# Vision tower on one core: the tokenizer's first two units reordered, its first weights in one transfer, and unread products in five waits of TensorE

## The chip, the cores and the metric

The program runs on one core of a Trainium2 chip. The metric is the device time of one execution in microseconds (us). The core's engines are named as the profile names them: PE is TensorE (PEld its weight loads), DVE is VectorE, ACT is ScalarE, POOL is GpSimd, SP is SyncE, which here only issues transfers. Each engine works through its own list of instructions in order, and waits on semaphores for the others.

## The reference

128 images of 128 x 128 pixels pass through a tokenizer and two transformer layers, all in float32:

```python
# tokenizer
x = _bn(_conv(X, w1, 8), g1, b1, m1, v1)      # 8x8, stride 8, 64 channels
x = _bn(_conv(x, w2, 2), g2, b2, m2, v2)      # 4x4, stride 2, 256 channels
# layer 0, attention
diff = Qg - Kg
attn = jnp.einsum('bqkgd,d->bqkg', jax.nn.relu(diff), w_mlp) + b_mlp[0]
attn = jax.nn.softmax(jax.nn.relu(attn), axis=2)
# layer 0, 4 experts of attention, weighted by a softmax gate
attn = jax.nn.softmax(jnp.einsum('bcehtd,bcehsd->bcehts', q, k) * scale, axis=-1)
# layer 1, linear attention
attn_weights = jnp.einsum('bhnd,bhmd->bhnm', jax.nn.softmax(q, axis=-1), jax.nn.softmax(k, axis=-2))
# layer 1, 8 experts, one per token, at most C = 1280 tokens each
idx = jnp.argmax(probs, axis=-1)
hmid = jax.nn.relu(jnp.einsum('ecd,edf->ecf', buf, w1) + b1[:, None, :])
ybuf = jnp.einsum('ecf,efd->ecd', hmid, w2) + b2[:, None, :]
```

The four parts of the layers read a layer norm of h, and each is added to h.

The output has 128 x 64 tokens of 256 features. The tokenizer's output is reordered into an image and cut into patches, which fixes where each of its results is stored.

## The kernel before

The kernel runs six stages one after the other: `tokenizer` (lines 62 to 257), `relu_attention` (260 to 727), `expert_attention` (730 to 1081), `linear_attention` (1084 to 1436), `route` (1495 to 1617), which sorts tokens by expert, and `experts` (1620 to 1797). The activations `h2` stay in SBUF through the first three stages and go to DRAM (`hd`) at the end of the third.

**Order of the work.** A part of the code that stands under `with tc.manual_schedule():` keeps the written order on each engine. What stands outside such a region, all of `route` for example, is put in order by a planner, which gives an engine the first instruction, in the written order, that its own reckoning holds ready. Two regions that follow one another, as those of the blocks in `experts` do, keep their own order inside, and the planner decides how they interleave. Semaphores are added by the framework from what each instruction reads and writes; a tile buffer taken again waits for the last reader of what was in it.

**The tokenizer.** An image row of 8 pixel lines is one tile `xt` (512 KB); there are 16, loaded three ahead. `conv1(r)` multiplies row r by `w1bd`, the 64 x 64 first weights twice on the diagonal, in two products of 512 columns (L130), each into one of two PSUM buffers `pa`. ACT takes the first to `ev` (two instructions, L135), DVE the second to `h` (L132). `differences(r)` makes two more tiles of `h` on DVE (L141, L142). `between(m, i, k)` makes a tile `v`: minus a row on ACT (L151) where there is no row above, else the difference of two rows (L154). A `Unit(m, ab)` is one of 16 groups of results (row group m, 64 channels ab). It has three `products(i)`: 24 matmul instructions each (L177), then ACT (L189) and DVE (L200 or L204); `results(k)` writes `h2` (L210). Products 0 need v(m,0,0) and v(m,0,1), products 1 need rows 4m+1 and 4m+2, products 2 need v(m,2,0) and v(m,2,1). The second weights `w` come in two transfers of 512 KB on ACT's queue; POOL and ACT make sums and negatives of them (L223, L226, L227). Scales and offsets of the batch norms come from `bnv1` and `bnv2` (L107 to L111). Before the change rows 0 to 4 pass first, then units 0 to 15, each behind one more row while there are rows:

```python
            for r in range(5):
                conv1(r)
                ...
                differences(r)
            ...
            for m in range(4):
                for ab in range(4):
                    ...
                    if r < 16:
                        conv1(r)
                    u.products(0)
```

**The places of the unread products.** In `relu_attention` the last step of the last block ends with scores (L297), then a maximum, exponents, sums and weights on DVE, ACT and POOL (L521 to L535), then transposes on PE (L544), a copy (L552), and products with v in two halves (L441) with copies (L452) and transposes back (L459). At the start of `linear_attention` a group `x` of tokens is loaded (L1131), its statistics are taken (L1139, L1140, then POOL), and ACT normalises it in place:

```python
                nc.scalar.activation(
                    self.x[:, j], self.x[:, j], AF.Identity, bias=self.nb[:, j : j + 1], scale=self.rs[:, j : j + 1]
                )
```

PE then transposes it (L1159), and the products for queries and keys follow (L1182). In `route` PE transposes the logits `lgs` (L1533), waits while DVE finds each token's expert and counts (up to L1553), makes two small products `pp` (L1555, L1556), waits again, and makes 64 products `pi` in eight groups (L1604), for which DVE makes `lh` and `hv` (L1594, L1597; two buffers each) and ACT scales `hv` (L1602). In `experts` the tokens of a block are gathered by POOL's indirect transfers (L1681), normalised (L1691 to L1699), transposed (L1712, copied to `xt` by L1715), and multiplied by `w1` (L1724) and `w2` (L1740), block after block.

Of the kernel before, what the change touches and what calls it, by code (L numbers as in the profile page):

```python
# [19 lines left out]
P = 128  # L20
# [11 lines left out]
class Ctx:  # L32
# [12 lines left out]

    def tables(self, const):


        self.rin = const.tile([P, NTILE], I32, name="rin")
        self.rout = const.tile([P, NTILE], I32, name="rout")  # L50
        self.bexp = const.tile([P, NBLK + 1], I32, name="bexp")
# [10 lines left out]
def tokenizer(c, x, w1, bn1, w2, bn2):  # L62
# [6 lines left out]
    with (  # L69
# [16 lines left out]
        nc.vector.memset(w1bd, 0.0)  # L86
        bnv1 = wp.tile([P, 4], F32, name="bnv1")
        bnv2 = wp.tile([P, 4, 4], F32, name="bnv2")
        for k in range(2):
            nc.sync.dma_start(w1bd[k * 64 : (k + 1) * 64, k * 64 : (k + 1) * 64], w1)  # L90
            nc.sync.dma_start(bnv1[k * 64 : (k + 1) * 64, :], bn1)
# [8 lines left out]
        for k in range(2):  # L100
            nc.scalar.dma_start(bnv2[k * 64 : (k + 1) * 64], bn2)
# [44 lines left out]
        def between(m, i, k):  # L146
# [5 lines left out]
            else:  # L152
                eng = nc.vector if (m, k) == (0, 1) else nc.gpsimd
# [65 lines left out]
        with tc.manual_schedule():  # L219
            for r in range(5):  # L220
                conv1(r)
                if r == 1:
                    nc.gpsimd.tensor_add(w[:, :, 1], w[:, :, 0], w[:, :, 2])  # L223
                differences(r)
                if r == 1:
                    nc.scalar.mul(w[:, :, 2], w[:, :, 2], -1.0)  # L226
                    nc.gpsimd.tensor_add(w02, w[:, 0:2], w[:, 2:4])  # L227
                    between(0, 0, 0)
                elif r == 2:
                    between(0, 0, 1)  # L230
            for k in range(2):
                between(0, 2, k)
            s2, o2 = scale_offset(lambda i: bnv2[:, i, :], [P, 4], "2")
            n2 = wp.tile([P, 4], F32, name="n2")
            nc.vector.tensor_scalar_mul(n2, s2, -1.0)
            for m in range(4):
                for ab in range(4):
# [22 lines left out]
def relu_attention(c, wqkv, wmlp, bmlp):  # L260
# [8 lines left out]
    with (  # L269
# [387 lines left out]
        with tc.manual_schedule():  # L657
# [63 lines left out]
            old.weights()  # L721
            old.transpose()
# [361 lines left out]
def linear_attention(c, hd, hx, out, lgs, sth, wqk, bqk, wv, bv, wgb):  # L1084
# [6 lines left out]
    with (  # L1091
# [313 lines left out]
        with tc.manual_schedule():  # L1405
            for g in range(4):
                groups[g].load()
            for g in range(3):
# [86 lines left out]
def route(c, k, gfd):  # L1495
# [5 lines left out]
    with (  # L1501
# [54 lines left out]
        nc.tensor.matmul(pp[:, 1], k.ones, cs[:, T - 1, :], start=True, stop=True)  # L1556
        nc.vector.tensor_reduce(gf, sq, AX.X, ALU.add)
# [62 lines left out]
def experts(c, hx, gfd, out, w1, w2, b2, routing):  # L1620
# [9 lines left out]
    with ExitStack() as nest:  # L1630
# [138 lines left out]
        with tc.manual_schedule():  # L1769
            for n in range(2):  # L1770
                blocks[n].load()
            for n in range(2):
                blocks[n].gather((False,))
            blocks[0].moments()
# [49 lines left out]
def layout(**i):  # L1824
# [9 lines left out]
    o["w1"] = i["L0_tok_w1"].reshape(64, 64)  # L1834
    o["bn1"] = np.stack([i[f"L0_tok_{k}1"] for k in "gbmv"], axis=1)
# [5 lines left out]
    o["bn2"] = bn2.reshape(4, 8, 2, 8, 2).transpose(1, 3, 0, 2, 4).reshape(64, 4, 4)  # L1841
# [48 lines left out]
```

## Time and profile before

| what | value |
|---|---|
| median of 3 runs | 2775.22 us (2774.36 to 2785.34) |
| the profiled execution's own time | 2783.14 us |
| span of its profile (first to last instruction) | 2781.3 us |
| mean granted clock of PE | 0.965 |
| PE busy | 2609.6 us (94%) |
| PEld busy | 1748.0 us (63%) |
| DVE busy | 2036.5 us (73%) |
| ACT busy | 1627.1 us (59%) |
| POOL busy | 1628.1 us (59%) |

By stretches of the span, PE is busy and its clock is granted as follows:

| stretch, us | stage | PE busy, us | granted clock |
|---|---|---|---|
| 0 to 180 | tokenizer | 164.51 | 0.97 |
| 180 to 1114 | relu_attention | 906.48 | 0.99 |
| 1114 to 1948 | expert_attention | 806.37 | 0.98 |
| 1948 to 2284 | linear_attention | 297.88 | 0.92 |
| 2284 to 2346 | route | 28.58 | 0.52 |
| 2346 to 2781 | experts | 405.79 | 0.96 |

All times inside the execution are counted from the start of the span. A row of the timeline gives the start, the duration, the engine, the line, the operation and its tiles, how many instructions were merged, and in brackets how long the engine had been idle and what ended that. The granted clock is the share of full speed at which the profile shows PE running. A float32 product appears as two matmul instructions.

### The profile page before, as it was taken

Reading aid. Unit: us, or ns where it says so; the run is one execution under the profiler, and the core shown is the slowest. Engines: PE = TensorE matmul, PEld = TensorE weight load, DVE = VectorE, ACT = ScalarE, POOL = GpSimd, SP = SyncE. Lnnn points to the kernel's source line nnn. Section 1 sums busy time; section 2 is a strip of 40 time slices with the busy share of each in tenths; the row PEclk is TensorE's granted clock in tenths of the full one; section 3 lists DMA queues with packets and bytes.
Section 4 is the critical chain, followed back from the end, with each engine's and each line's share of the span. In section 5 each row is a group of like instructions: output and inputs, shape, how many; then the busy total and the mean of one; then the engine's idle time right before and its main releaser. Section 6 shows DMA issues by size and latency. Waiting matters only on the chain. (4 is left out here: it accounts for less than half of the span.)

```text
span 2781.3 us, 76925 instructions
## 1 busy us (share of the span) xinstructions
PE 2609.6 (94%) x33260; PEld 1748.0 (63%) x33260; DVE 2036.5 (73%) x3017; ACT 1627.1 (59%) x3411; POOL 1628.1 (59%) x1389
## 2 busy tenths in 40 slices
PE   7989999999999998899999999998899965999997
PEld 3553444444444443688888888887466645888886
DVE  6759999999998997577777777776467755444443
ACT  3228889888888887466665666565354432233332
POOL 3329888888888887765566565643133211454444
PEclk9999999999999999899999999999899975999999
DMA  3000000000000000000000000000444433555554
GB/s 107 31 12 1 2 1 2 1 2 2 1 2 1 2 2 2 12 11 18 11 18 11 11 18 11 18 11 17 115 89 109 101 90 109 173 191 190 194 194 133
DMA packets 138063, 140.80 MB, mean 51 GB/s; under 512 B 107923, under 2 KB 121509, under 8 KB 130032
## 3 DMA queue, kind: packets, MB, share of 16 engines
q1 hardware_dynamic: 126816, 117.91, 14.2%
q0 software_dynamic: 7648, 14.77, 1.7%
q8 instruction: 263, 4.31, 0.6%
q10 hardware_dynamic: 3248, 3.09, 0.4%
q14 instruction: 88, 0.72, 0.1%
HBM read 103.93 MB, written 32.54 MB: 49 GB/s over the span
## 5 line engine op out<-in xcount | busy, mean ns | idle before, releaser
L495 POOL TENSOR_TENSOR m<-q,k 128x1024 f32<-128x1024 f32 x384 | 719.0, 1903 | 30.5 <-PE sc L297 16.1
L487 DVE TENSOR_TENSOR m<-pc,k 128x2048 f32<-128x2048 f32 (+1 forms) x320 | 646.7, 2058 | 0.5 <-ACT q L431 0.5
L297 PE MATMUL sc<-m,wide 128*32 128x512 f32 x4096 | 529.6, 598 | 12.0 <-DVE m L487 7.1
L496 ACT ACTIVATE m<-m 128x1024 f32<-128x1024 f32 x384 | 402.2, 1049 | 5.9 <-POOL m L495 5.2
L297 PEld LDWEIGHTS sc<-m,wide 128*32 128x32 f32 x4096 | 126.4, 109 | 259.7 <-issue 146.2
L505 ACT ACTIVATE m<-k,q 128x64 f32<-128x64 f32 x1024 | 270.9, 339 | 0.8 <-DVE k L378 0.8
L946 DVE TENSOR_REDUCE mx<-sc 128x16 f32<-128x1024 f32 x128 | 156.1, 1220 | 154.7 <-PE sc L934 131.9
L961 POOL TENSOR_TENSOR e<-e,mx 128x1024 f32<-128x1024 f32 x128 | 243.4, 1902 | 10.1 <-POOL mx L960 0.2
L906 ACT COPY qk<-pqk 128x512 f32<-128x512 f32 x256 | 139.0, 605 | 134.3 <-PE pqk L902 134.3
L960 POOL TENSOR_TENSOR mx<-mx,gate 128x16 f32<-128x16 f32 x128 | 27.6, 216 | 316.9 <-ACT z L991 153.2
L1724 PE MATMUL ph<-xt,w1s 128*128 128x256 f32 x896 | 203.3, 386 | 3.4 <-DVE xt L1715 3.0
L1740 PE MATMUL po<-w2s,hT 128*128 128x256 f32 x896 | 198.0, 379 | 0.0
L973 ACT COPY pT<-pt 128x512 f32<-128x512 f32 x256 | 138.8, 600 | 98.9 <-PE pt L970 98.1
L1724 PEld LDWEIGHTS ph<-xt,w1s 128*128 128x128 f32 x896 | 173.3, 194 | 29.2 <-DVE xt L1715 3.8
L1740 PEld LDWEIGHTS po<-w2s,hT 128*128 128x128 f32 x896 | 168.1, 190 | 21.7
L902 PE MATMUL pqk<-xT,w 64*128 64x128 f32 x2048 | 169.5, 289 | 2.7 <-issue 2.7
L947 DVE TENSOR_TENSOR e<-sc,mx 128x1024 f32<-128x1024 f32 x128 | 156.8, 1225 | 4.4
L1728 ACT ACTIVATE hT<-ph,w1s 128x256 f32<-128x256 f32 x224 | 93.3, 470 | 106.6 <-PE ph L1724 106.6
L1758 POOL DMA_INDIRECT out<-y,rout x56 | 56.7, 1013 | 168.6 <-ACT hT L1728 125.1
L953 DVE TENSOR_REDUCE mx<-e 128x16 f32<-128x1024 f32 x128 | 153.3, 1198 | 2.5 <-ACT e L950 2.4
L902 PEld LDWEIGHTS pqk<-xT,w 64*128 64x128 f32 x2048 | 142.3, 189 | 20.4 <-issue 11.1
L970 PE MATMUL pt<-ident,e 128*128 128x128 f32 x1024 | 142.9, 280 | 5.0 <-POOL e L961 1.5
(290 smaller groups left out, 4986.7 us busy)
## 6 DMA issues: line engine op xcount, KB each, us to landing
w1s<-in_we SPq DMA_DIRECT2D x30, 1028.0 KB, 5.3
w2s<-in_we SPq DMA_DIRECT2D x30, 1024.0 KB, 5.0
hd<-h SPq DMA_DIRECT2D x16, 512.0 KB, 3.2
x<-hd SPq DMA_DIRECT2D x16, 512.0 KB, 3.9
h<-hd SPq DMA_DIRECT2D x4, 2048.0 KB, 12.7
hx<-h SPq DMA_DIRECT2D x4, 2048.0 KB, 11.4
out<-h SPq DMA_DIRECT2D x4, 2048.0 KB, 20.6
xt<-in_x SPq DMA_DIRECT2D x15, 512.0 KB, 3.5
```

The source lines that it names most:

```text
L297: nc.tensor.matmul(dst[j : j + 32], wide[:, hf, s : s + 32], part, start=start, stop=stop)
L487: nc.vector.tensor_tensor(m, bcast(self.pq[:, hf, i : i + n], 3, T), k, ALU.max)
L495: nc.gpsimd.tensor_tensor(m, bcast(self.q[:, hf, s : s + 2], 3, T), k, ALU.subtract)
L496: nc.scalar.activation(m, m, AF.Relu)
L505: nc.scalar.activation(self.parts[i, hf][:, q], self.blk.k[:, hf, i], AF.Relu, bias=self.q[:, hf, i - NB // 2, q : q + 1], scale=-1.0,)
L902: nc.tensor.matmul(pq[par][:, k, eh, :], w[r, f : f + P], self.xT[r, fc], start=True, stop=True)
L946: nc.vector.tensor_reduce(mx, sc, AX.X, ALU.max)
L947: nc.vector.tensor_sub(e, sc, bcast(mx, 2, T))
L953: nc.vector.tensor_reduce(self.sm[x], self.e[x], AX.X, ALU.add)
L961: nc.gpsimd.tensor_mul(e, e, bcast(sm, 2, T))
L1724: nc.tensor.matmul(ph[:, j], self.w1[:, w0 : w0 + P], self.xt[:, fc], start=(fc == 0), stop=(fc == 1))
L1740: nc.tensor.matmul(po, self.hT[:, f, r * P : r * P + P], self.w2[:, f, :], start=(f == 0), stop=(f == 7))
```

## The change

A helper `busy(out, x, n)` multiplies the identity by x n times into a PSUM tile that nobody reads. It is called in five places: 4 products ahead of the tokenizer's first unit, 9 ahead of the last transposes of `relu_attention`, 6 at the start of `linear_attention`, 7 in `route` behind `pp`, and 12 at the start of `experts`. In the tokenizer the order is written out anew: units 0 and 1 begin after row 2, and rows 3 to 6 and the parts of the two units alternate. One of the differences of rows moves from DVE to POOL. The first weights arrive as a full 128 x 128 matrix laid out by the host, in one transfer and without a memset, `bn1` and `bn2` in one transfer each, and `bn2` on SP's queue.

```diff
@@ -42,6 +42,11 @@
         nc.vector.memset(self.nhalf, -0.5)
         self.zero = const.tile([P, 8], F32, name="zero")
         nc.vector.memset(self.zero, 0.0)
+
+    def busy(self, out, x, n):
+
+        for _ in range(n):
+            self.nc.tensor.matmul(out, self.ident, x, start=True, stop=True)
 
     def tables(self, const):
 
@@ -83,12 +88,10 @@
 
 
         w1bd = wp.tile([P, P], F32, name="w1bd")
-        nc.vector.memset(w1bd, 0.0)
         bnv1 = wp.tile([P, 4], F32, name="bnv1")
         bnv2 = wp.tile([P, 4, 4], F32, name="bnv2")
-        for k in range(2):
-            nc.sync.dma_start(w1bd[k * 64 : (k + 1) * 64, k * 64 : (k + 1) * 64], w1)
-            nc.sync.dma_start(bnv1[k * 64 : (k + 1) * 64, :], bn1)
+        nc.sync.dma_start(w1bd, w1)
+        nc.sync.dma_start(bnv1, bn1)
         load(0, nc.scalar)
         for r in range(1, 3):
             load(r)
@@ -97,8 +100,7 @@
         w02 = wp.tile([P, 2, 3, D], F32, name="w02")
         for k in range(2):
             nc.scalar.dma_start(w[:, :, 2 * k, :], w2[k].rearrange("k p c -> p k c"))
-        for k in range(2):
-            nc.scalar.dma_start(bnv2[k * 64 : (k + 1) * 64], bn2)
+        nc.sync.dma_start(bnv2, bn2)
 
         def scale_offset(bnv, shape, name):
 
@@ -150,7 +152,7 @@
             if r < 0:
                 nc.scalar.mul(v, parts[r + 2], -1.0)
             else:
-                eng = nc.vector if (m, k) == (0, 1) else nc.gpsimd
+                eng = nc.vector if (m, i, k) == (0, 0, 1) else nc.gpsimd
                 eng.tensor_sub(v, parts[r], parts[r + 2])
             taken[m, i, k] = v
 
@@ -217,24 +219,46 @@
                 )
 
         with tc.manual_schedule():
-            for r in range(5):
-                conv1(r)
-                if r == 1:
-                    nc.gpsimd.tensor_add(w[:, :, 1], w[:, :, 0], w[:, :, 2])
-                differences(r)
-                if r == 1:
-                    nc.scalar.mul(w[:, :, 2], w[:, :, 2], -1.0)
-                    nc.gpsimd.tensor_add(w02, w[:, 0:2], w[:, 2:4])
-                    between(0, 0, 0)
-                elif r == 2:
-                    between(0, 0, 1)
-            for k in range(2):
-                between(0, 2, k)
+            conv1(0)
+            conv1(1)
+            nc.gpsimd.tensor_add(w[:, :, 1], w[:, :, 0], w[:, :, 2])
+            differences(0)
+            nc.scalar.mul(w[:, :, 2], w[:, :, 2], -1.0)
+            differences(1)
+            nc.gpsimd.tensor_add(w02, w[:, 0:2], w[:, 2:4])
+            between(0, 0, 0)
+            conv1(2)
+            differences(2)
+            between(0, 0, 1)
             s2, o2 = scale_offset(lambda i: bnv2[:, i, :], [P, 4], "2")
             n2 = wp.tile([P, 4], F32, name="n2")
             nc.vector.tensor_scalar_mul(n2, s2, -1.0)
+
+            c.busy(ps1.tile([P, 4, B], F32, tag="pa", name="idle"), w[:, 0, 0:2], 4)
+            units = [Unit(0, ab) for ab in range(2)]
+            units[0].products(0)
+            conv1(3)
+            units[0].products(1)
+            differences(3)
+            units[0].results(0)
+            between(0, 2, 0)
+            conv1(4)
+            units[1].products(0)
+            differences(4)
+            between(0, 2, 1)
+            units[1].products(1)
+            units[1].results(0)
+            conv1(5)
+            units[0].products(2)
+            units[0].results(1)
+            differences(5)
+            between(1, 0, 0)
+            conv1(6)
+            units[1].products(2)
+            units[1].results(1)
+            differences(6)
             for m in range(4):
-                for ab in range(4):
+                for ab in range(0 if m else 2, 4):
                     u = Unit(m, ab)
                     r = 4 * m + 5 + ab
                     if r < 16:
@@ -719,6 +743,7 @@
             old.exponents()
             old.sums()
             old.weights()
+            c.busy(psq.tile([P, 8, T], F32, tag="pq", name="idle"), blocks[-1].k[:, 0, 0:8], 9)
             old.transpose()
             old.transposed()
             for n in range(len(seq), len(seq) + 12):
@@ -1405,6 +1430,7 @@
         with tc.manual_schedule():
             for g in range(4):
                 groups[g].load()
+            c.busy(psp.tile([P, 2, D], F32, tag="pp", name="idle"), groups[0].x[:, 0:2], 6)
             for g in range(3):
                 for i in range(NG):
                     groups[g].statistics(i)
@@ -1554,6 +1580,8 @@
         pp = gpp.tile([P, 2, E], F32, name="pp")
         nc.tensor.matmul(pp[:, 0], k.before, cs[:, T - 1, :], start=True, stop=True)
         nc.tensor.matmul(pp[:, 1], k.ones, cs[:, T - 1, :], start=True, stop=True)
+        idle = gpp.tile([P, 4, B], F32, name="idle")
+        c.busy(idle, k.lgs[:, 0], 7)
         nc.vector.tensor_reduce(gf, sq, AX.X, ALU.add)
         nc.vector.reciprocal(gf, gf)
         nc.scalar.dma_start(gfd.rearrange("(p t) o -> p (t o)", p=P), gf)
@@ -1771,6 +1799,7 @@
                 blocks[n].load()
             for n in range(2):
                 blocks[n].gather((False,))
+            c.busy(psh.tile([P, 2, BLK], F32, tag="ph", name="idle"), blocks[0].w1[:, 0:512], 12)
             blocks[0].moments()
             blocks[0].normal()
             blocks[0].transpose()
@@ -1831,14 +1860,17 @@
     ev, od = x[:, :, :, 0::2], x[:, :, :, 1::2]
     x = [np.concatenate(y, axis=2) for y in ((ev[:, 0], od[:, 0]), (od[:, 1], ev[:, 1]))]
     o["x"] = np.concatenate(x, axis=1)
-    o["w1"] = i["L0_tok_w1"].reshape(64, 64)
-    o["bn1"] = np.stack([i[f"L0_tok_{k}1"] for k in "gbmv"], axis=1)
+
+    o["w1"] = np.zeros((P, P), np.float32)
+    for k in range(2):
+        o["w1"][k * 64 : k * 64 + 64, k * 64 : k * 64 + 64] = i["L0_tok_w1"].reshape(64, 64)
+    o["bn1"] = np.tile(np.stack([i[f"L0_tok_{k}1"] for k in "gbmv"], axis=1), (2, 1))
 
     w2 = i["L0_tok_w2"].reshape(4, 4, 64, 8, 2, 8, 2).transpose(0, 1, 2, 4, 6, 3, 5).reshape(4, 4, 64, D)
     o["w2"] = np.stack([w2[:, 1::-1], w2[:, 3:1:-1]]).reshape(2, 4, P, D)
     bn2 = np.stack([i[f"L0_tok_{k}2"] for k in "gbmv"], axis=0)
 
-    o["bn2"] = bn2.reshape(4, 8, 2, 8, 2).transpose(1, 3, 0, 2, 4).reshape(64, 4, 4)
+    o["bn2"] = np.tile(bn2.reshape(4, 8, 2, 8, 2).transpose(1, 3, 0, 2, 4).reshape(64, 4, 4), (2, 1, 1))
     q, k, v = (i[f"L0_attn_W{n}"].T for n in "qkv")
 
     v = v.reshape(D, 32, 8).transpose(0, 2, 1).reshape(D, D)
```

## Prediction

> **What bounds the kernel now.** I read the stretches first (start and end, length, busy time and instructions of PE, PEld, DVE, ACT and POOL, granted PE clock, DMA share, GB/s), because products that nobody reads can act on the clock alone:
>
> ```profile
> 0.00:34.00 34.00, 18.59 (x23) 6.35 (x24) 15.75 (x23) 11.55 (x13) 12.04 (x16) 0.85 0.43 144
> ...
> 1098.00:1116.00 18.00, 8.55 (x308) 7.04 (x304) 7.49 (x21) 3.36 (x6) 2.89 (x9) 0.81 0.05 11
> 1948.00:1966.00 18.00, 6.63 (x16) 3.82 (x17) 6.70 (x27) 5.21 (x10) 6.75 (x24) 0.53 0.61 203
> 2283.00:2310.00 27.00, 1.38 (x8) 1.17 (x8) 19.49 (x81) 0.63 (x1) 0.00 (x0) 0.57 0.31 77
> 2318.00:2346.00 28.00, 27.59 (x128) 27.38 (x128) 13.44 (x15) 16.62 (x64) 0.00 (x0) 0.50 0.59 226
> 2346.00:2362.00 16.00, 7.46 (x20) 5.83 (x21) 5.31 (x18) 0.84 (x2) 12.16 (x14) 0.51 0.15 41
> 2362.00:2764.00 402.00, 398.33 (x1890) 349.30 (x1888) 177.20 (x414) 120.14 (x278) 196.53 (x225) 1.00 0.55 185
> ```
>
> In the last row, which is nearly all of `experts`, PE is busy 99% at full clock: there it is the bound, and a later start is a later end. The other rows are the surroundings of the five places. The largest piece of work at half clock is `pi` in `route`, 27.59 us of PE in 2318 to 2346. The waits of PE (total, times, longest) name what ends each place's wait:
>
> ```profile
> PE pp L1555 <- DVE cs L1553: 25.6, 1, 25.6
> PE pt L1159 <- ACT x L1150: 14.6, 4, 6.0
> ...
> PE pi L1604 <- ACT hv L1602: 8.1, 1, 8.1
> PE pt L1712 <- DVE xn L1699: 7.9, 1, 7.9
> ...
> PE pt L544 <- POOL e L535: 4.6, 1, 4.6
> ```
>
> Then the timeline of the tokenizer's start:
>
> ```profile
> 16.07 0.81 DVE L132 TENSOR_SCALAR h<-pa,s,o 128x512 f32<-128x512 f32 x1 [2.45 <-PE pa L130]
> 17.08 3.90 POOL L227 TENSOR_TENSOR w<-w 128x1536 f32<-128x1536 f32 x1 [4.87 <-ACT w L226]
> 17.63 3.91 DVE L142 TENSOR_TENSOR h<-h,ev 128x512 f32<-128x512 f32 x1
> 21.57 1.48 ACT L151 ACTIVATE v<-h 128x1536 f32<-128x1536 f32 x1 [4.56 <-DVE h L142]
> 34.73 2.81 PE L177 MATMUL pc<-v,w 128*64 128x256 f32 x24
> ```
>
> A 0.69 us difference on DVE takes 3.91 because POOL's L227 runs beside it. From 34.73 to 179.92 PE never stops, so that an earlier start of the units is worth only what it leaves less to do.
>
> **Prices.** A product of `busy` is two instructions 0.43 us apart at full clock, 0.86 a product (row 1.98 for 4, L130 at 42.65), and 1.71 at half (3.75 for 4 at 7.60; where one was cut by the clock, 0.85 an instruction). Full clock came back 3.3 us after PE began anew at 187.46 (granted from 190.8) and 6.1 us after 2355.63 (from 2361.7): I carry both ends. n products that begin at half clock take 0.86 n plus half the time to full clock, 1.7 to 3.1 us. All 38 run in front of real products on the same engine, so what outlasts a wait is delay.
>
> [...]
>
> **Tokenizer.** (a) `w1bd` goes first on SP, and `bnv1` second, at 1.41 after an issue of 0.61. Issue to landing was 2.9 to 5.6 for `bnv`, 4.5 to 5.4 for `w1bd`: I take bnv1 at 5.9 (5.2 to 6.3). Scales took 1.39 (7.74 to 9.13), the table load 1.28, `ev` 1.57: row 0 is on ACT until 10.3, before 12.08. (b) Row 1 at half clock: 1.71 to 12.05, ev until 13.65, L226 (1.06) until 14.75, L227 3.90 until 18.65: 2.3 earlier than the 20.98 of before. (c) Both rows' differences now stand behind row 1's L132 at 13.8, so that L227 catches the second of four; three end behind it, one every 0.6: 20.45. L151 until 22.0, row 2's ev until 23.6 (24.65 before). (d) The 4 unread products need the PSUM buffer that this ev frees, and PE has been idle since 17.2: they run 23.6 to 28.7 or 30.1. I take 29.5. The last `v` (h2, d2, 1.76) is ready at 26.7, so they outlast their wait by 2.8; without them the first unit would start at half clock and lose 1.7 to 3.1 itself. (e) Before, six rows were through at 34.73; now three, and a row between units costs 9.83 - 7.77 = 2.06 (unit with a row, 42.65 to 52.48, and without, 138.31 to 146.08). Break-even is 34.73 - 6.2 = 28.55: **+0.95**. (f) v(0,2,1) moves from DVE (1.76) to POOL (3.44) and stands behind v(0,2,0) there. From 29.5: unit 0's second product ends at 36.7, z 38.3, row 3's differences 39.5, POOL until 43.4 (with 0.4 lost to L210), row 4's differences, blocked until then, 44.6, POOL until 48.1. PE wants it at 46.0 (29.5 + 4 x 2.59 + 3 x 2.06): **+2.1**, with all later units queued behind it on PE. Sum **+3.1**; bounds +0.6 (clock still full at 23.6, start 27.1, same wait) and +4.0 (bnv1 at 6.3, slow return of the clock). At nothing: the memset (DVE idle until 7.74), two issues less on ACT (idle until 9.21), `bnv2` on SP behind rows 1 and 2 (first read at 26.8; the next issue there is row 3's, at 11.38 before). Without that cover each would cost its issue, 0.6.
>
> **relu_attention, 9 products.** They start at 1098.1 at full clock: 7.7 us, until 1105.8. The transposes were released at 1102.89. At full clock L552 follows them after 1.19 (1095.24 to 1096.43): 1107.0 for 1104.91. The first half of L441 takes 1.48 (row at 332.80) for 2.12. **+1.5** (0.9 if the second half gains too, 2.1 if nothing does); the next stage's memsets wait for the last L459.
>
> **linear_attention, 6 products.** They read the group that ACT normalises in place, so L1150 waits for the sixth: a wait added, with four normalisations, the transposes and L1160 behind it. Start 1955.3 (x landed), length 5.2 + 1.7 to 3.1: until 1962.2 to 1963.6 instead of L1150 at 1959.67. L1182 goes from 1962.94 to 1965.5 to 1966.9; at full clock, where before 2.86 us (until 1965.8) ran at half, worth 1.43. **+1.7** (2.5; 0 if the three later waits of L1159 for ACT, 8.6 us, swallow it).
>
> **route, 7 products.** `route` is ordered by the planner. It takes what is ready:
>
> ```profile
> 2293.68 0.82 DVE L1523 TENSOR_REDUCE var<-sth 128x64 f32<-128x512 f32 x1
> 2294.41 0.19 DVE L1519 TENSOR_SCALAR mean<-mean 128x64 f32<-128x64 f32 x1
> ...
> 2305.21 0.69 DVE L1557 TENSOR_REDUCE gf<-sq 128x64 f32<-128x512 f32 x1
> 2305.82 0.68 DVE L1548 TENSOR_REDUCE m<-oh 128x64 f32<-128x512 f32 x1
> ```
>
> L1557 is written behind `pp` (L1555) and runs 4 us ahead of it. The unread products need `lgs` alone, ready at 2278; I expect them right behind the transposes, 2283.6 to 2289.6, in the middle of a wait of 25.6 us: **0**, the clock is down again long before 2318. This is the point the time hangs on most.
>
> **experts, 12 products.** They begin at 2345.9, at half clock: 10.3 + 1.7 to 3.1, until 2357.9 to 2359.3; the transposes were released at 2353.76. Then 0.60 for 1.08 and 7.07 (row at 2391.37) for 10.16: the first hidden layer ends at 2366.2 to 2367.6 instead of 2365.79. Behind it PE waited 2.19 us at 2375.32 for `xt` (gathers that POOL issues one after the other), which covers that; and the wait cost the next L1724 8.86 for 7.07. With PE later this wait is too short to drop the clock: **-1.5** (-3.6 if the later load of w1 also lets the gather land sooner; +1.0 if the clock drops all the same).
>
> **The sum**: 3.1 + 1.5 + 1.7 + 0 - 1.5 = +4.8. The profiled execution's 2783.14 (span 2781.3 and 1.8 around it) would become 2787.9. It lies 7.9 above the median of 2775.22, one of whose runs was 2785.34; from the median the sum gives **2780**. Its bounds, -2.1 and +9.6, give 2773 to 2785. About 0.5%, 13.9 us, is what a measurement of this kernel can tell from no change: I forecast no change.
>
> **Rivals.**
> - *The products of route stay behind pp.* They would end at 2317.5 to 2318.9, with the clock full as `pi` begins. Its groups then go by DVE, ACT and two buffers (1.95 + 2.06 + 0.5 over 2, 2.28) instead of 3.42: eight end at 2336.2 for 2345.85, -9.6, and the 12 start at full clock, 10.3 for a wait of 8.0: -1.0. Sum -4.3: 2771 (bound -11.7, 2763.5). For it: the written place. Against: L1557.
> - *Both, and the tokenizer without its waits*: start at 27.1 and no wait in (f) is -1.4; with -9.6, -3.6 and places two and three at 0, 2760.6. Needs four ends at once.
> - *Slower.* The 12 products make the planner's PE late, and it puts the gather's statistics ahead of `xt` in more blocks. One such wait costs 2.19 and 1.8 at half clock, 4.0 together; with +4.8 it passes 13.9 from 3 of the 28 blocks left, and 8 give 2812. Against: L1715 delays L1724 in only two of 29 blocks.
> - *The unread products are dropped in compilation.* Then only the tokenizer counts, start 26.7 with 1.7 to 3.1 lost and the wait of (f): +2.7, 2778.
>
> **How the numbers follow.** Forecast 0.69; route in order 0.15; both 0.04; slower 0.06; dropped 0.06. 2766 to 2786 leaves out "both", "slower" and the tails of the first two, at most 0.2 together. Faster by over 0.5% takes the 0.04 and a tail, 0.06; slower the 0.06 and a tail, 0.07; the rest is within.
>
> **What would show it.** Right: the first L177 near 29.5, a PE wait for POOL's L154 of some 2 us near 46, L544 near 1105.8, L1150 near 1963, the products of route before 2290, a granted clock of 0.5 through `pi`, a full one from 2362 on. Wrong: `pi` at full clock, no wait near 46, or waits of L1724 for L1715 past 2400.

## The result and the profile after

The changed kernel has a median of 2790.5 us (16 runs, 2785.4 to 2796.0). The kernel before, with more runs than the three that were known when the prediction was made, has a median of 2782.7 us (16 runs, the three among them). The ratio is 1.0034, with a 95% interval from 1.0025 to 1.0043: slower, by less than the 0.5% that the prediction counted as a change. The forecast "no change" held by that bound; the predicted time of 2780.0 did not, and 2790.5 lies 4.5 us above the top of its range. The profiled execution of the changed kernel took 2789.33 us (span 2787.6), that of the kernel before 2783.14 (span 2781.3).

Line numbers have moved: by 2 in the first half of the tokenizer, by 24 to 28 from `relu_attention` on; `busy` is L49. The stretches of the kernel after, with the columns as before:

```profile
0.00:34.00 34.00, 22.54 (x78) 9.37 (x80) 15.68 (x26) 11.87 (x15) 9.62 (x16) 0.95 0.41 142
...
1948.00:1968.00 20.00, 11.59 (x26) 5.62 (x27) 6.81 (x28) 3.43 (x7) 7.04 (x25) 0.66 0.48 160
...
2324.00:2352.00 28.00, 27.48 (x129) 27.29 (x129) 13.41 (x17) 16.23 (x63) 0.00 (x0) 0.50 0.58 220
2352.00:2366.00 14.00, 13.64 (x28) 5.95 (x28) 2.83 (x10) 0.00 (x0) 9.12 (x10) 0.81 0.13 38
2366.00:2770.00 404.00, 400.41 (x1904) 351.00 (x1904) 178.85 (x421) 120.52 (x280) 199.86 (x228) 1.00 0.55 185
```

The first row shows a clock of 0.95 where it was 0.85. The third shows `pi` unchanged, 27.5 us at 0.50. The fourth is the wait ahead of `experts`, now full of unread products, and the last says that PE is the bound behind it, as before. The waits of PE:

```profile
PE pp L1581 <- DVE cs L1579: 20.5, 1, 20.5
PE pt L1184 <- ACT x L1175: 9.9, 7, 4.0
...
PE pi L1632 <- ACT hv L1630: 8.1, 1, 8.1
```

The wait ahead of `pp` is 5 us shorter, that ahead of `pi` is what it was: the products of `route` went to the front of the first one, between and behind the transposes of the logits. The timeline of the tokenizer's start (start, duration, engine, line, operation):

```profile
13.97 3.86 POOL L228 TENSOR_TENSOR w<-w 128x1536 f32<-128x1536 f32 x1 [1.17 <-ACT w L226]
14.48 3.90 DVE L144 TENSOR_TENSOR h<-h,ev 128x512 f32<-128x512 f32 x1
...
19.20 5.37 PE L49 MATMUL idle<-w,ident 128*128 128x512 f32 x8 [4.89 <-issue]
...
24.50 2.81 PE L179 MATMUL pc<-v,w 128*64 128x256 f32 x24
...
43.38 2.38 PE L179 MATMUL pc<-v,w 128*64 128x256 f32 x20 [1.67 <-POOL v L156]
```

The last of the four differences that stood in a row is caught by POOL's sum, as expected: it begins behind the sum and takes 3.90 us where one takes 0.68. The unread products start as soon as DVE has emptied a buffer (19.11), not when ACT has; the first unit starts at 24.50, and near 43 PE waits for POOL's second `v`. The two places that cost most of the rest:

```profile
1955.94 8.12 PE L49 MATMUL idle<-x,ident 128*128 128x512 f32 x12 [1.30 <-DMA x<-hd]
1964.80 0.33 PE L1184 MATMUL pt<-ident,x 128*128 128x128 f32 x1 [0.74 <-ACT x L1175]
...
1967.28 7.13 PE L1207 MATMUL pq<-w,xT 128*128 128x512 f32 x16 [0.24 <-ACT xT L1185]
...
2351.98 13.23 PE L49 MATMUL idle<-w1s,ident 128*128 128x512 f32 x24 [0.52 <-PE pi L1632]
```

Read as a ledger against the one trace of before, start against start: the tokenizer ends 2.1 us earlier; the stage behind `relu_attention` starts 0.6 later (+2.7); the first L1207 starts 4.3 later than the first L1182 did; `route` starts 5.6 later, `pi` 5.6 later, the end comes 6.3 later. The experiments showed that such a ledger of two single traces misleads by several us.

### The profile page after: what moved, and what is told of

Read it like the earlier page. It is cut to its first block, busy times and chain, and to the rows that moved or that the text cites. A ratio compares the mean times of both kernels' runs of the same rounds, so it can differ in the third digit from the quotient of the medians.

```text
span 2787.6 us, 77062 instructions
## 1 busy us (share of the span) xinstructions
PE 2634.8 (95%) x33336; PEld 1756.3 (63%) x33336; DVE 2035.3 (73%) x3015; ACT 1627.6 (58%) x3411; POOL 1634.0 (59%) x1390
## 5 line engine op out<-in xcount | busy, mean ns | idle before, releaser
L1752 PE MATMUL ph<-xt,w1s 128*128 128x256 f32 x896 | 199.0, 380 | 3.2 <-ACT hT L1756 1.6
L1752 PEld LDWEIGHTS ph<-xt,w1s 128*128 128x128 f32 x896 | 169.8, 190 | 28.0 <-ACT hT L1756 2.9
```

The source lines that it names most:

```text
L1752: nc.tensor.matmul(ph[:, j], self.w1[:, w0 : w0 + P], self.xt[:, fc], start=(fc == 0), stop=(fc == 1))
```

## The experiments

The expectations name theories by a letter: P is a term of the prediction, T the reading of that ledger, H two thresholds of the clock, W the offset of its windows (both the author's assumptions then; what the traces show of them stands in the last section), Q a meeting of POOL and DVE; the others are described where they stand. The median and the range are those of the kernel's runs; the ratio is to the kernel before, run beside them. Its median was 2781.9 us beside `tok_alone`, `places_alone`, `route_late` and `no_linear`, 2779.5 beside `no_experts` and the three `doses`, 2778.2 beside `no_relu` and `transfers_only`, 2782.2 beside the four `warm` kernels and 2779.3 beside the last two. The changed kernel's 2790.5 stood beside 2782.7, so that differences to it are good to some 3 us; where they matter, each median is also taken against that of the kernel before beside it.

**1. The tokenizer alone, and the four later places alone.** `tok_alone` drops the four later calls:

```diff
-            c.busy(psq.tile([P, 8, T], F32, tag="pq", name="idle"), blocks[-1].k[:, 0, 0:8], 9)
-            c.busy(psp.tile([P, 2, D], F32, tag="pp", name="idle"), groups[0].x[:, 0:2], 6)
-        c.busy(idle, k.lgs[:, 0], 7)
-            c.busy(psh.tile([P, 2, BLK], F32, tag="ph", name="idle"), blocks[0].w1[:, 0:512], 12)
```

> The changed kernel without the four later sets of unread products (9, 6, 7 and 12), so the tokenizer's part of the change alone. Theory T (the trace of after is the measure): PE leaves the tokenizer near 177.8 instead of 179.9, about 2 us are won and kept, so 1.7 to 2.1 us less than the kernel before, ratio 0.9993; relu_attention's last transposes begin near 1101.2 and pi runs at half clock as before. Theory P (my prediction's term): 3.1 us more than before, ratio 1.0011. Theory C (chance): places at the end of linear_attention where the clock drops or not differ from run to run by up to 3 us either way, so the time may lie 3 us to either side of T while the tokenizer's own end still shows 177.8.

Measured: 2783.0 (2775.4 to 2786.2), ratio 1.0007, interval 0.9996 to 1.0018, which is +1.9 us, from -1.1 to +5.0. P's +3.1 lies inside, T's -2 outside, although the trace of this kernel again ends the tokenizer 2.3 us ahead of before's. `places_alone` has the tokenizer of before and the four later calls:

> The kernel before with the four later sets of unread products, the tokenizer as before. T: relu_attention +2.0, start of linear_attention +2.7, route 0, experts +0.7, so 5.4 us more than before, ratio 1.0019; up to 3 us more or less by the clock at the end of linear_attention. P: +1.5, +1.7, 0, -1.5, so 1.7 us more, ratio 1.0006. The unread products of route run before 2290 and pi at a granted clock of 0.50 by both.

Measured: 2784.1 (2780.5 to 2792.7), ratio 1.0019, interval 1.0005 to 1.0032: +5.3 us, from +1.4 to +8.9 (+2.2 by the medians). That is near T's 5.4, but P's 1.7 lies inside too.

**2. One place left out.** `no_linear`, `no_experts` and `no_relu` are the changed kernel without one of the lines above.

> The changed kernel without the six unread products of linear_attention. T: the first L1207 begins at the time of before plus what stands ahead of it (near 1963.2) instead of 1967.3, its first 16 take 8.5 instead of 7.1, so 2.7 us less than the changed kernel (up to 3 us more or less by the clock at the end of linear_attention). P: 1.7 less. A third theory, that the later start only shifts later waits for ACT: within 1 us of the changed kernel.

Measured: 2787.2 (2783.3 to 2790.4), 3.3 less than the changed kernel; ratio 1.0027, interval 1.0013 to 1.0041.

> The changed kernel without the 12 unread products of experts. T (trace of after): the first L1752 begins at pi's end plus 9.8 as before, at half clock, the first hidden layer takes 10.2 and the second waits for xt as before: 0.7 us less than the changed kernel. P: 1.5 us more. Rival: the later load of PE changes the order of DVE's work in the blocks behind, and the time moves by more than 3 us either way.

Measured: 2787.7 (2784.8 to 2792.2), 2.8 less; ratio 1.0030, interval 1.0016 to 1.0044. P's 1.5 more is not seen.

> The changed kernel without the nine unread products of relu_attention. T: the last transposes start 3 us earlier but at half clock, the stage ends 2.0 us earlier relative to its start: 2 us less than the changed kernel's 2790.4. P: 1.5 less. Rival: the stage behind starts with waits for its weights and for POOL, which take it back: within 0.7 us of the changed kernel.

Measured: 2786.7 (2784.4 to 2790.7), 3.8 less; ratio 1.0029, interval 1.0017 to 1.0040. But with each median taken against the kernel before beside it, the three are 2.5 less, 0.5 more and 0.7 more than the changed kernel, and the intervals of the ratios overlap its own, 1.0025 to 1.0043. By the times, none of the three places is shown to cost anything; for two of them the stages below show it.

**3. The products of route behind pp.** In `route_late` they are written into the buffer of `pp`, so that they must wait for its readers:

```diff
-        pp = gpp.tile([P, 2, E], F32, name="pp")
+        big = gpp.tile([P, 4, B], F32, name="pp")
+        pp = big[:, 0, 0 : 2 * E].rearrange("p (a e) -> p a e", a=2)
...
-        c.busy(idle, k.lgs[:, 0], 7)
...
         nc.vector.tensor_add(cs, cs, bcast(pp[:, 0], 1, T))
+        c.busy(big, k.lgs[:, 0], 5)
```

> The changed kernel with five unread products of route in place of seven, written into the PSUM buffer of pp, so that they cannot run before DVE has read pp. They start near 2316.6, last 4.3 to 8.5 us, and pi begins near 2324. Theory H (the clock has two thresholds: kept at full while PE does some 0.4 of its possible column work in a window of 3.4 us, regained only above about 0.8): pi, which does 0.61 of it at half clock and would do about 0.46 when DVE sets its pace, stays at full clock: 27.6 becomes 18 to 20 us, and the 12 products behind it take 10.3 instead of 13.2, so 10 to 13 us less than the changed kernel, near 2779, ratio to before 0.9985. Rival: one threshold between 0.61 and 0.8 for both ways: the clock falls within pi after one window, pi takes 24 us or more, at most 4 us less than the changed kernel.

Measured: 2777.7 (2776.1 to 2782.6), 12.8 less than the changed kernel (12.0 with each against the kernel before beside it); ratio to before 0.9993, interval 0.9983 to 1.0004. Its timeline:

```profile
2319.49 6.16 PE L49 MATMUL pp<-lgs,ident 128*128 128x512 f32 x10 [0.89 <-DVE cs L1601]
...
2326.66 4.22 PE L1632 MATMUL pi<-hv,lh 128*128 128x78 f32 x32 [1.01 <-ACT hv L1630]
...
2340.75 5.85 PE L1632 MATMUL pi<-hv,lh 128*128 128x78 f32 x32 [0.48 <-ACT hv L1630]
```

Two groups of `pi` take 4.22 plus a wait of 0.48 where they took 6.9, and the whole of it 19.95 us where it took 27.59. Only in the last of four pairs did the clock fall (5.85), behind a window in which PE passed columns for 0.37 of the time; the windows before it had 0.42 to 0.51. That is H, and it is the prediction's first rival, with its -9.6 near enough.

**4. Smaller doses.** `doses` is `route_late` with 4 products in `relu_attention`, none in `linear_attention` and 6 in `experts`:

```diff
-            c.busy(psq.tile([P, 8, T], F32, tag="pq", name="idle"), blocks[-1].k[:, 0, 0:8], 9)
+            c.busy(psq.tile([P, 8, T], F32, tag="pq", name="idle"), blocks[-1].k[:, 0, 0:8], 4)
-            c.busy(psp.tile([P, 2, D], F32, tag="pp", name="idle"), groups[0].x[:, 0:2], 6)
-            c.busy(psh.tile([P, 2, BLK], F32, tag="ph", name="idle"), blocks[0].w1[:, 0:512], 12)
+            c.busy(psh.tile([P, 2, BLK], F32, tag="ph", name="idle"), blocks[0].w1[:, 0:512], 6)
```

> The changed kernel with other numbers of unread products: 4 in relu_attention (9 before), none in linear_attention, 5 in route behind pp's readers, 6 in experts (12). Theory H (two thresholds, full clock kept with some 0.4 of the column work in each window of 3.4 us): 4 products keep the clock in relu_attention and end before POOL's e at 1101.6, so its last transposes start 3 us earlier than in the changed kernel at full clock; without linear's six 2.7 us are won; six in experts end within the wait of 7.9 us, so the first transposes start 3 to 4 us earlier than with 12. Against route_late (2777.7) that is some 8 us, near 2770, ratio to before 0.9955. Rival: PE is late anyway for DVE's xt and later waits take it back: as route_late, 2776 to 2778.

Measured: 2772.8 (2769.4 to 2777.4), 4.9 less than `route_late` (2.5 less when the median of each is taken against that of the kernel before beside it); ratio 0.9983, interval 0.9973 to 0.9992. Less than H's 8, and hardly more than the rival's 0 to 2. `doses_old_tok` puts the tokenizer of before into it:

> As doses, but with the tokenizer and its input layouts of the kernel before. T: PE leaves the tokenizer 1 to 2.3 us later than in doses, so 1 to 2 us more than doses. P (my term): 3.1 us less than doses. Rival from the timed tok_alone (1.0007, from 0.9996 to 1.0018 of before): 2 us less than doses, the tokenizer's gain being given back in the stage behind it.

Measured: 2771.1 (2760.6 to 2773.1), in two groups, three runs up to 2766.0 and four from 2771.1; ratio 0.9956, interval 0.9940 to 0.9972. T fell here: its trace ends the tokenizer 3.6 us later than that of `doses`, and its times are not longer. The median is 1.7 less and the mean 4.7 less than that of `doses`, so that P's 3.1 less and the rival's 2 less cannot be told apart. `doses_no_tok_products` drops the four products ahead of the first unit:

> As doses, without the four unread products ahead of the tokenizer's first unit. H: PE has been idle since row 2 and the clock is at half, so the first unit starts near 24.7, when its last v is ready, and runs at half clock for one to two windows: 1.7 to 3.4 us more than doses, all of it seen at the end of the tokenizer. Rival: the clock does not fall or comes back as early as with the products: within 0.5 us of doses.

Measured: 2773.3 (2771.1 to 2775.0), ratio 0.9979, interval 0.9970 to 0.9987. Its trace ends the tokenizer 3.5 us later, as H expected; the medians differ by 0.4. The profiled execution of `doses` was the fastest of its twelve runs and this one the slowest of twelve, so that the pair of traces exaggerates; the four products are worth nothing that these runs can tell.

**5. The two groups of times of the kernel before.** `transfers_only` is the kernel before with only the new input layouts and transfers:

> The kernel before with nothing but the new transfers of w1, bn1 and bn2 (order of rows and units, differences and places as before). T: PE starts near 4.9 instead of 7.6 and the first unit 2 to 2.7 us earlier, so 2 us less than before, which would make the transfers the source of all that the tokenizer wins, and the new order worth nothing. Rival O: POOL's sums of w wait for the second weights as before, the first unit starts near 34.7 all the same, and the new order is the source.

Measured: 2778.7 (2772.4 to 2784.2), ratio 0.9996, interval 0.9984 to 1.0008; first unit at 32.62. The 2.1 us at the first unit are as T said, nothing is left of them at the end that can be told. `before_again` and `before_b` are the kernel before, unedited, for its trace:

> The kernel before, for a second trace of it. Its 33 executions beside the first experiments lie in two groups, nine from 2772.8 to 2775.3 at a mean granted clock of 0.966 to 0.967 and most of the others from 2780 to 2787 at 0.963 to 0.966. Theory W: the clock is granted in windows of 3.41 us whose offset to the program differs between executions, so short waits of PE fall into one window or two; then the traces differ in which waits drop the clock, by two to five windows, and in nothing else. Rival: the work itself differs, transfers or engines taking longer in one stage.

> The kernel before, for a third trace of it, to the same question as the second: W expects the stages' differences to follow the windows at half clock (half of each window's length), the rival a stage that is longer at the same granted clock.

Measured: 2777.7 and 2770.8 us, one run each. Both traces start the first unit at 27.1 and 27.0 us, not at 34.73. The timeline of the second:

```profile
15.69 0.68 DVE L142 TENSOR_TENSOR h<-h,ev 128x512 f32<-128x512 f32 x1
...
15.99 3.67 POOL L227 TENSOR_TENSOR w<-w 128x1536 f32<-128x1536 f32 x1 [3.74 <-ACT w L226]
...
27.01 2.81 PE L177 MATMUL pc<-v,w 128*64 128x256 f32 x24
```

Here the clock was full from 10.9 on, rows 1 and 2 passed at full speed, and L142 of row 1 began 0.3 us ahead of POOL's sum and took 0.68. In the trace that the prediction was made from it began 0.55 behind (17.63 after 17.08) and took 3.91; the rows stopped, the clock fell from 23.6 to 33.8, and the unit started 7.7 us later. W's first half is right (which windows are at half differs), the rival's too (one stage is longer). That these starts make the two groups of whole times is not shown: `before_again` started early as well and took 2777.7.

**6. The clock made certain.** `before_warm` gives PE work from 1.5 us on, before its first data:

```diff
+            c.busy(ps2.tile([P, 4, 4, N], F32, tag="pc", name="idle")[:, 0, 0:2].rearrange("p o n -> p (o n)"), c.ident, 12)
             for r in range(5):
                 conv1(r)
```

> The kernel before with 12 unread products of 128 columns (the identity by itself) ahead of the first row, while PE waits 6 us for its first data. Theory W: the clock is full as the first row begins, whatever the offset of its windows, so every execution is like the two early traces (first unit at 27.0): one group of times near 2773, none from 2780 to 2787, mean 6 to 7 us less than before's 2780, ratio 0.9975. Rival: the two groups have another cause and stay, mean within 2 us of before.

Measured: 2784.8 (2782.0 to 2786.9), ratio 1.0013, interval 1.0002 to 1.0024. One group as W said, but the late one; W's price was wrong by 12 us. Its timeline:

```profile
7.86 1.96 PE L135 MATMUL pa<-xt,w1bd 128*128 128x512 f32 x4 [1.41 <-DMA w1bd<-in_w]
...
15.12 3.46 POOL L233 TENSOR_TENSOR w<-w 128x1536 f32<-128x1536 f32 x1 [2.62 <-ACT w L232]
15.22 3.91 DVE L147 TENSOR_TENSOR h<-h,ev 128x512 f32<-128x512 f32 x1
...
30.84 2.81 PE L182 MATMUL pc<-v,w 128*64 128x256 f32 x24
```

Row 0 runs at full speed (1.96 for 3.75), and the difference comes 0.1 us behind POOL's sum instead of 0.3 ahead. With the clock full as row 0 begins, the first unit is 3.8 us later than in `before_b`, so that the meeting on DVE, with what it sets off, is worth about half of the 7.7 us. The same 12 products in `doses_old_tok` (`warm_old`), 7 in `doses` (`warm_new`), and `warm_old` with a fourth place:

```diff
+            c.busy(psp.tile([P, 2, D], F32, tag="pp", name="idle"), w[:, 0], 4)
             for g in range(3):
                 for i in range(NG):
                     groups[g].statistics(i)
```

> As doses_old_tok with the 12 early products. W: only the fast group of doses_old_tok is left (2760.6 to 2766.0), mean near 2763, ratio 0.9940. Rival: as doses_old_tok, 2768 in the mean with two groups.

> As doses (new order) with 7 early products, as its first row starts 2.7 us sooner. W: the first unit starts at most 1.5 us earlier than in doses (24.3), for its last v, and three rows are still to come: it ends the tokenizer 4 us behind warm_old, mean near 2771. T (the new order wins 2.1 us at the tokenizer's end): 2 us less than warm_old.

> As warm_old with four unread products at the start of linear_attention that read the weights w, not the group x that ACT normalises in place. If that wait was the loss: they run from 1.0 us behind w's landing, end before x is normalised, the transposes start as without them, and the first 16 L1182-like products take 7.1 instead of 8.5: 1.4 us less than warm_old. Rival: unread products there cost by their own length, whatever they read: 2 us more than warm_old.

Measured: `warm_old` 2771.6 (2769.8 to 2774.1), ratio 0.9963, interval 0.9949 to 0.9977; `warm_new` 2773.3 (2770.5 to 2774.7), 0.9965, interval 0.9953 to 0.9977; `warm_old_lin` 2770.5 (2768.3 to 2773.6), 0.9960, interval 0.9945 to 0.9974. W fell for the first of them too: its difference is caught as well (15.01 after 14.91 us), and the two orders cannot be told apart then. In `warm_old_lin`, beside the wait of 9.2 us for the weights, the place reads:

```profile
1955.03 6.53 PE L49 MATMUL idle<-w,ident 128*128 128x512 f32 x8 [0.26 <-DVE wsum L1467]
1961.39 0.69 PE L1166 MATMUL pt<-ident,x 128*128 128x128 f32 x3
...
1963.25 7.13 PE L1189 MATMUL pq<-w,xT 128*128 128x512 f32 x16 [0.24 <-ACT xT L1167]
```

Nothing waits for a normalisation that the products hold up: the transposes follow at once, and the 16 products take 7.13 (8.52 in the trace of before). From the end of `expert_attention` to the first transpose of the logits in `route` it is 1.4 us less than in `warm_old`, as expected; the times (1.1 less) cannot confirm so little.

**7. The meeting taken away.** In `sum_on_dve` the sum moves from POOL to DVE, behind row 2's `h`, in the kernel before; `best` does the same in `warm_old_lin`:

```diff
                 conv1(r)
+                if r == 2:
+                    nc.vector.tensor_add(w02, w[:, 0:2], w[:, 2:4])
...
-                    nc.gpsimd.tensor_add(w02, w[:, 0:2], w[:, 2:4])
```

> The kernel before with one step moved: the sum w02 (128 x 1536), on POOL behind row 1, goes to DVE behind row 2's h, where the two early traces show DVE idle from 17.7 to 19.6. Theory Q (the meeting of POOL's sum with DVE's second difference of row 1 decides): no difference takes 3.9 us any more, the first unit starts between 27 and 30 us in every execution, one group of times, 2773 to 2777, mean 5 us less than before's 2780. Rival W (the clock's windows decide): the two groups stay, mean within 2 us of before. Third: the 1.8 us on DVE delay row 2's differences and the first unit by as much, no gain.

> warm_old_lin with the sum w02 on DVE as in sum_on_dve. Q: the first unit near 25 to 27 us instead of 30.4, nothing falls to half clock before 175 us, 4 to 6 us less than warm_old_lin's 2770.8 in the mean: 2765 to 2767, ratio to before 0.9945. W: as warm_old_lin.

Measured: `sum_on_dve` 2778.9 (2773.6 to 2782.1), ratio 0.9997, interval 0.9982 to 1.0011; first unit at 27.29, no difference of row 1 caught, and one group. But its mean, 2778.7, is 1.4 below before's 2780.1 and not 5; Q's price is not shown for this kernel. `best`: 2766.1 (2763.6 to 2772.3), ratio 0.9954, interval 0.9940 to 0.9968, 4.4 less than `warm_old_lin`, as Q said, but 1.5 less when each is taken against the kernel before beside it, and the intervals overlap; Q's price is not shown here either. Its first unit is 4.1 us earlier than in the trace of `warm_old_lin` (26.31 for 30.39). `best` is faster than both kernels: by 13 us than the kernel before beside it, and by 21 than the changed kernel with each against the kernel before. Its tokenizer:

```profile
14.99 0.68 DVE L147 TENSOR_TENSOR h<-h,ev 128x512 f32<-128x512 f32 x1
...
16.53 1.75 DVE L229 TENSOR_TENSOR w<-w 128x1536 f32<-128x1536 f32 x1
...
26.31 2.81 PE L182 MATMUL pc<-v,w 128*64 128x256 f32 x24
```

**The stages over all traces.** With 20 traces, each stage can be compared between all kernels that have an edit in it and all that have not. Lengths in us, from PE's first instruction of one stage to that of the next (`linear_attention` from the last product of the stage ahead, `experts` from the end of `pi` to the end of the span):

| stage | variant | mean (lowest to highest), traces |
|---|---|---|
| tokenizer, until `relu_attention` starts | order of before | 179.8, 179.8, 187.3, 187.5, 188.7 |
| | new order, products for the first unit | 185.9 (185.1 to 186.9), 7 |
| relu_attention | none | 930.4 (929.2 to 932.2), 8 |
| | nine | 932.2 (931.6 to 933.8), 5 |
| | four | 932.1 (930.0 to 934.0), 7 |
| end of relu_attention, from its last but one group of transposes (L544) until `expert_attention` starts | none | 21.5 (21.2 to 21.9), 8 |
| | nine | 23.7 (23.2 to 24.7), 5 |
| | four | 21.8 (21.0 to 23.0), 7 |
| expert_attention, until its last product ends | no edit in it | 826.2 (822.7 to 828.7), 20 |
| linear_attention | none | 339.2 (337.5 to 340.2), 13 |
| | six that read x | 342.3 (341.2 to 343.7), 5 |
| | four that read w | 336.3 (336.1 to 336.6), 2 |
| route | none, or seven early | 64.2 (64.1 to 64.6), 12 |
| | five behind pp | 55.2 (55.0 to 56.5), 8 |
| experts | none | 434.7 (432.7 to 436.2), 8 |
| | twelve, from half clock | 435.3 (434.8 to 436.2), 4 |
| | six, from full clock | 432.6 (431.0 to 433.5), 7 |

The terms of the change read so: tokenizer +1.3 (against the mean of the five), `relu_attention` +1.9, `linear_attention` +3.1, `route` 0, `experts` +0.6, 6.9 in all. The times give 7.8 by the medians and 9.4 (7.0 to 12.0) by the ratio. For `linear_attention` and `route` the ranges of the variants do not overlap; for the other whole stages they do, and 0.9 to 2.5 us have no place. `expert_attention`, which no kernel edits, differs by 6 us between the traces, so that so little cannot be placed. The end of `relu_attention` alone, 23.7 us long with the nine products and 21.5 without, shows their cost free of the rest of the stage: 2.2 us, and the ranges do not overlap. Four products there cost nothing that can be told and won nothing.

## Why the prediction was wrong

- **The base, the step that failed.** The sum was right in size, +4.8 against 7 to 9, but was put on 2775.22, the median of three runs of which two came from the faster of its groups of times. The profiled execution's own 2783.14 + 4.8 = 2787.9 stands in the prediction; the median of 16 runs, 2782.7, agrees with it, and with it the bounds of the sum (-2.1 to +9.6) would have been 2780.6 to 2792.3, and held. Of the 10.5 us missed, 7.5 are this step. The other 3.0 are, by the table, `linear_attention` 1.4, `experts` 2.1 and `relu_attention` 0.4 too low and the tokenizer 1.8 too high, 2.1 together; 0.9 has no place. The three runs shown, 2774.36, 2775.22 and 2785.34, were two groups and no centre.
- **Tokenizer.** The first L177 was put at 29.5 and came at 24.50, for two reasons. Row 1 was costed at half clock, and the clock was full from 9.0 (1.98 for 3.78). And the unread products were made to wait for ACT's `ev` (23.6), though they got the buffer that DVE's `h` frees (19.11). The rows for it were in the trace of before, where row 3's first product waits for DVE's L132 and only its second for ACT:

```profile
22.31 1.12 PE L130 MATMUL pa<-xt,w1bd 128*128 128x512 f32 x2 [3.98 <-DVE h L132]
...
24.70 3.78 PE L130 MATMUL pa<-xt,w1bd 128*128 128x512 f32 x4 [1.27 <-ACT ev L135]
```

Point (c), L227 catching a difference, was right, and (f) too: 1.67 for 2.1. But +3.1 stood against a trace whose first unit starts at 34.73; in two other traces of the same kernel it starts at 27.1 and 27.0. Against the one the new order gains 2.1 us, against the others it loses 5.5 to 6. So the term came out near what the times allow (+1.9, from -1.1 to +5.0) by a working that was wrong at both ends; that is luck.

- **relu_attention.** Right in kind, a little low: +1.5, measured +1.9 over the whole stage and +2.2 at its end; the transposes at 1104.39, which with the 1.7 us that this trace was ahead is 1106.1 for 1105.8.
- **linear_attention.** The added wait on the normalisation was named rightly and sized too low, +1.7 for +3.1. The products began 0.6 later than assumed and took 8.12, near the upper bound of 8.3; the 1.4 us won at full clock came as computed, 7.13 for the 8.52 of before:

```profile
1962.94 8.52 PE L1182 MATMUL pq<-w,xT 128*128 128x512 f32 x16
```

- **route.** Right: the planner moved them to 2287.75 to 2294.36, between and behind the transposes, and `pi` stayed at half clock. The rival's -9.6, had they stayed behind `pp`, measured -9.0.
- **experts.** -1.5 became +0.6. The cover was there at first: relative to the end of `pi` the second hidden layer ended 0.9 earlier than before (2388.69 - 5.60 against 2384.02). Three blocks on, at 2433.97 - 5.60 against 2427.65, it was 0.7 later: L1752 waited 0.36 and 1.27 us for `hT` where one wait of 0.45 stood before. The longest wait after the change, and the one before:

```profile
2432.14 1.99 PE L1752 MATMUL ph<-xt,w1s 128*128 128x256 f32 x8 [1.27 <-ACT hT L1756]
```

```profile
2425.82 1.99 PE L1724 MATMUL ph<-xt,w1s 128*128 128x256 f32 x8 [0.45 <-ACT hT L1728]
```

The step that failed in this term is that a gain at PE would last. Why ACT's `hT` came later there was not tried.

- **The other rivals.** The unread products were not dropped: all 38 are in the trace, as 76 instructions. No wait of L1752 for L1743 above 1 us came after 2376, so the slower rival's mechanism did not occur.
- **The clock in `pi`.** The prediction took the row of `pi` as it stood, 27.59 us of PE at 0.50, and expected 0.5 again. In the trace of after PE was busy for 27.48 of the 28 us from 2324 to 2352, at 0.50, so the row was right. With what share of the columns `pi` goes at half and at full clock stands in the last section.

## What to carry to other kernels

Here unread products paid where their wait outlasted them and they left its end alone: five behind `pp` (`route` 55.2 us for 64.2) and four in `linear_attention` that read w (336.3 for 339.2). Six there that read x held up its normalisation and cost 3.1 us. So look what else writes the tile they read, whether a planner may move them (the seven of `route` ran ahead of `pp` and won nothing), and at which clock the work behind them starts: `pi` took 27.59 us from half clock and 19.95 from full (`route_late`). Before a change of a few us is costed, get the times of many runs and more than one trace of the kernel before: one trace was one draw out of two groups 7.7 us apart in its first stage. And compare stages over all traces that share an edit, since a single pair put the tokenizer at -2.1 where the times of `tok_alone` allow -1.1 to +5.0.

## What the runs showed of the hardware

**The granted clock, and what PE did ahead of its changes.** All changes of the granted clock in a trace lie on a grid of 3.413 us, to 0.01 us. Its offset differs between executions: 3.10 us from the span's start in the trace of before, 2.20 in that of after, 1.84 in `tok_alone`, 2.74 in `places_alone`, 1.69 in `route_late` and 1.04 in `no_linear`. A window is here one step of that grid. For each I took the share in which PE passes columns (a column counted as 0.83 ns at full clock, from 512 columns in 0.43 us, and twice that at half, from 0.853), in all windows of the 20 traces in which no product of a part of the array ran, 4298 of them:

| clock in the window | share of the window | next window at full, at half |
|---|---|---|
| full | below 0.35 | 0, 159 |
| full | 0.35 to 0.40 | 37, 12 |
| full | 0.40 and more | 3481, 0 |
| half | below 0.75 | 0, 461 |
| half | 0.75 to 0.80 | 11, 2 |
| half | 0.80 and more | 135, 0 |

Some windows come in, drop out or change their row with the way products that lie across an edge are shared out; the two bounds stay.

In these traces the full clock was kept behind every window with a share of 0.40 or more (3481) and behind none below 0.35 (159). It came back behind every window at half with 0.80 or more (135) and behind none below 0.75 (461). These are counts over this kernel and its variants; what sets the clock was not shown. `pi`, with 78 columns for each load of weights, has 0.61 at half clock and stays there, though PE is busy for 27.48 of 28 us in the trace of after. At full clock, where it waits 0.48 us for ACT between pairs of groups (`route_late`), it has 0.37 to 0.52 and stays full in seven of eight traces; in `route_late` the clock fell behind its window of 0.37.

**Who comes first, by 0.1 us.** A difference of 128 x 512 on DVE takes 0.68 us, and 3.90 to 3.91 where it begins 0.10 us (`before_warm`, 15.22 for 15.12) to 0.55 us (before, 17.63 for 17.08) behind POOL's sum of 128 x 1536. 0.3 us ahead of it (`before_b`, 15.69 for 15.99) it takes 0.68, and in the changed kernel's trace 0.1 us ahead too (L143 at 13.88, POOL's sum at 13.97). A delayed one ends some 0.55 us behind POOL's sum: at 21.54 for 20.98 in the first trace of before, at 19.13 for 18.58 in `before_warm`. With the sum on DVE (`sum_on_dve`) the difference of row 1 takes 0.69 at 15.96. By what means POOL's sum holds it was not shown. That making the kernel's start faster (`before_warm`) turned the early case into the late one was not expected; that it did so in every execution is argued from its eleven times, which lie together, and from one trace.
